# A four-layer transformer chain on one core: attention scores in tiles of three banks and one, keys spread by transfers, half of a modulation on two other engines

## The chip, the cores and the metric

The kernel runs on one NeuronCore of a Trainium2 chip. TensorE (PE in the profile; its weight loads are PEld) does the matrix products, VectorE (DVE), ScalarE (ACT) and GpSimd (POOL) the rest, and SyncE (SP) issues nearly all transfers (DMAs). Matrix products land in PSUM, which the kernel divides into banks of 512 float32 values on 128 partitions; everything else lies in SBUF. Each engine works through its own instructions in order and waits on semaphores for the others; transfers issued by one queue are issued in the order of the program too. The metric is the device time of one execution in microseconds; lower is better. All data are float32.

## What is computed

The input `x` is 128 sequences of 64 tokens with 128 channels, beside a context of the same size and one condition vector for each sequence. Four layers follow one another. The first three are attention with 16 heads of 8 elements; the last one is a mixture of three experts.

```
L0:  x += gate * self_attend(ln(x)*(1+scale)+shift) @ Wp     # 'L0s'
     x += attend(q from ln(x), k and v from the context)@Wp  # 'L0c'
     x += gate * mlp(ln(x)*(1+scale)+shift)
L1:  x += attend(q from ada_ln(x), k, v from ada_ln(ctx))@Wp # 'L1c'
L2:  self attention 'L2s', cross attention 'L2c' (context normalised), mlp
L3:  mixture of experts with a router and a gate
attend: softmax(q k^T / sqrt(8)) v for each head, 64 queries by 64 keys
```

Scales, shifts and gates are linear functions of the condition; they differ from sequence to sequence.

## The kernel before

The 8192 tokens are 16 groups of 512 (8 sequences, called batches in the code); all of `x` stays in SBUF. Attention runs in stages over the groups: L0s and L0c, then the MLP of L0, then L1c, L2s and L2c, then the MLP of L2, then L3. In each attention stage a group goes through three generators whose pieces are interleaved by hand.

`prepare` (line 386) makes a group ready in pieces: load the context, statistics on DVE, normalisation on POOL (in L2c also four pieces `cn` on ACT, L413), a transposition of the normalised tokens by PE into a PSUM tile (`psT`, L342), their modulation or copying into SBUF (`modulated_by_batch`: eight ACT instructions of 64 columns, L359; `copied`, L379), then the key product `pk` (L436), the copy `kT`, and the spread keys `kbd`: four POOL instructions (L444), each multiplying kT by a column of `mask`, so that of each 32 partitions (four heads) only one head's 8 stay non-zero. Then the query product `pq` (L449) with its copy `qT`, and the values `pvv`, `vbd`.

`scores` (line 468) multiplies 32-partition pieces of qT with kbd into one PSUM tile `sc` of four banks, one bank for each four heads, for four batches of a group. DVE reduces it to maxima `mx` (L485) and subtracts them into `e` (L487). `turned` (line 493) transposes half of e by PE into `pp` (two banks, one buffer) and ACT takes the exponential into `eT` (L507); `weighted` multiplies with vbd into `po` (L520) and ACT copies the result to `o` (L528). One value column of vbd is ones, so that po also holds the sums. `finish` (line 530) sends the sums through DRAM to get reciprocals spread over the partitions (`sums`, `rc`, `recs`, `rb`), moves odd heads' results with four transfers `o<-o`, multiplies `oT` on POOL (L557), projects by PE (`py`, L563) and adds to x.

`attend` (line 571) orders it all: step k does the scores of half k, then turns and weighs halves k-1 and k-2, with the pieces of prepare and finish in between. The even step of a pair (u = 0) has on PE: sc, pp, po, pk, py, pp, psT. The odd one: sc, pp, po, pq, pp, pvv, and in cross attention a second psT for the queries. The tiles psT, pk, pq, pvv, po and py share two PSUM banks in turn (`mm`), so each waits until the one two before it has been read. In an attention stage sc has four banks, pp two and mm two, one buffer of sc and of pp.

## Time and profile before

Three runs took 1624.05, 1625.13 and 1627.65 us; the median is 1625.13. The profiled execution took 1626.31 us; its span from the first to the last instruction is 1624.5 us.

| | us | share of the span |
|---|---|---|
| PE busy | 1573.8 | 97% |
| DVE busy | 1240.4 | 76% |
| ACT busy | 1035.5 | 64% |
| POOL busy | 1072.5 | 66% |
| granted TensorE clock, mean | 0.997 | |

Busy time says how long an engine had an instruction under way; PE's ends are modelled, so a busy PE is not a PE at its peak. The groups of instructions give the number, the busy time and the mean duration, then the idle time of the engine before them and who ended it. The chain that ended last is followed back from the end: at each point the work that everything after it waited for.

### The profile page before, as it was taken

How to read it: one execution, taken by the hardware profiler on the slowest of the kernel's cores; microseconds unless marked ns; L12 is line 12 of the kernel's file. 1: busy time of each engine (PE TensorE's matmuls, PEld its weight loads, DVE VectorE, ACT ScalarE, POOL GpSimd, SP SyncE). 2: the span in 40 equal slices, each digit the busy share in tenths (PEclk: the TensorE clock that was granted, in tenths of full speed). 3: DMA queues.
4: the chain of work that ended last, by engine and by line, in shares of the span. 5: the costliest groups of instructions: out<-in, count | busy, mean ns of one | idle time of the engine just before them, and what ended most of it. 6: DMA issues, size and time to landing. Idle time of an engine off the chain costs nothing.

```text
span 1624.5 us, 64028 instructions
## 1 busy us (share of the span) xinstructions
PE 1573.8 (97%) x27842; PEld 1086.8 (67%) x27842; DVE 1240.4 (76%) x1566; ACT 1035.5 (64%) x1710; POOL 1072.5 (66%) x1786
## 2 busy tenths in 40 slices
PE   6999999998999899999999999998999999999998
PEld 4676777776544577776777777776777566666665
DVE  7898998898555688899899889896443566666666
ACT  5788777776433678878888888886334544444443
POOL 6687787766888789887787876775875333333322
PEclk9999999999999999999999999999999999999999
DMA  8334453332111022211334432222533111111100
GB/s 209 85 82 99 107 127 92 83 83 72 55 36 55 16 63 61 72 44 50 90 82 102 104 88 73 62 56 59 130 81 76 31 39 37 40 33 36 34 12 19
DMA packets 146775, 112.65 MB, mean 69 GB/s; under 512 B 36357, under 2 KB 125247, under 8 KB 146495
## 3 DMA queue, kind: packets, MB, share of 16 engines
q1 hardware_dynamic: 146288, 108.53, 26.1%
q8 instruction: 219, 3.59, 0.9%
q14 instruction: 61, 0.50, 0.1%
q10 hardware_dynamic: 207, 0.03, 0.0%
HBM read 83.99 MB, written 14.02 MB: 60 GB/s over the span
## 4 chain that ended last, share of the span: by engine, by line
PE 83%; DVE 12%; ACT 3%; issue 1%; DMA 0%; SPq 0%; DVEq 0%
PE sc L478 10%; PE pp L503 9%; PE po L520 7%; PE ph L693 7%; PE ph L1080 6%; PE ph L1081 6%; DVE e L487 6%; DVE mx L485 6%; PE po L1111 5%; PE psT L342 5%; PE pk L436 5%; PE py L563 4%; PE py L709 4%; PE py L699 3%; PE pvv L459 3%; PE pq L449 3%
## 5 line engine op out<-in xcount | busy, mean ns | idle before, releaser
L507 ACT ACTIVATE eT<-pp 128x1024 f32<-128x1024 f32 x320 | 329.7, 1030 | 160.8 <-PE pp L503 160.7
L485 DVE TENSOR_REDUCE mx<-sc 128x32 f32<-128x2048 f32 x160 | 366.6, 2291 | 83.6 <-PE sc L478 83.6
L487 DVE TENSOR_TENSOR e<-sc,mx 128x2048 f32<-128x2048 f32 x160 | 366.6, 2291 | 5.4
L503 PEld LDWEIGHTS pp<-ident,e 64*128 64x128 f32 x5120 | 183.9, 138 | 140.1 <-ACT eT L507 44.7
L503 PE MATMUL pp<-ident,e 64*128 64x64 f32 x5120 | 227.7, 229 | 7.2 <-DVE e L487 4.7
L444 POOL TENSOR_SCALAR kbd<-kT,mask 128x512 f32<-128x512 f32 x316 | 212.4, 690 | 31.3 <-ACT kT L438 28.3
L372 POOL TENSOR_SCALAR xn<-x,nmu,rs 128x128 f32<-128x128 f32 x508 | 223.6, 453 | 13.3
L557 POOL TENSOR_TENSOR oT<-o,rb 128x512 f32<-128x512 f32 x80 | 102.1, 1276 | 163.5 <-DMA rb<-recs 62.9
L478 PE MATMUL sc<-kbd,qT 32*64 32x256 f32 x5120 | 179.2, 387 | 16.6 <-DVE e L487 15.6
L694 ACT ACTIVATE h<-ph,vec 128x512 f32<-128x512 f32 x128 | 87.3, 687 | 149.9 <-PE ph L693 149.7
L520 PE MATMUL po<-eT,vbd 128*32 128x64 f32 x10240 | 178.1, 221 | 1.4 <-issue 1.3
L1087 ACT ACTIVATE h<-h 128x512 f32<-128x512 f32 x112 | 70.6, 630 | 149.8 <-DVE h L1083 130.9
L520 PEld LDWEIGHTS po<-eT,vbd 128*32 128x32 f32 x10240 | 151.3, 110 | 14.4 <-issue 2.0
L330 POOL TENSOR_TENSOR rs<-rs,nhalf 128x4 f32<-128x4 f32 x128 | 130.2, 1017 | 10.7
L478 PEld LDWEIGHTS sc<-kbd,qT 32*64 32x64 f32 x5120 | 97.7, 131 | 53.0 <-issue 19.6
L1083 DVE TENSOR_TENSOR h<-ph,ab 128x512 f32<-128x512 f32 x112 | 76.9, 687 | 62.6 <-PE ph L1081 62.5
L1116 DVE SCALAR_TENSOR_TENSOR acc<-po,pr,acc 128x128 f32<-128x128 f32 x192 | 67.2, 350 | 44.1 <-PE po L1111 39.6
L1080 PE MATMUL ph<-nx,w 128*128 128x512 f32 x192 | 100.7, 607 | 0.0
L528 ACT COPY o<-po 128x512 f32<-128x512 f32 x160 | 95.7, 598 | 5.1 <-PE po L520 2.0
L1081 PE MATMUL ph<-u,w_ev 128*128 128x512 f32 x192 | 98.9, 597 | 0.0
L1111 PEld LDWEIGHTS po<-w_2o,h 128*128 128x128 f32 x768 | 92.1, 192 | 8.7 <-issue 8.4
L1104 POOL TENSOR_SCALAR g<-g 128x512 f32<-128x512 f32 x16 | 9.9, 622 | 132.1 <-ACT g L1103 132.1
(259 smaller groups left out, 2868.5 us busy)
## 6 DMA issues: line engine op xcount, KB each, us to landing
rb<-recs SPq DMA_DIRECT2D x80, 256.0 KB
c<-in_ctx_dram SPq DMA_DIRECT2D x64, 256.0 KB
o<-o SPq DMA_DIRECT2D x320, 32.0 KB
gt<-gate_L_xcond_sa_proj_w SPq DMA_DIRECT2D x32, 256.0 KB
gt<-gate_L_xcond_W_proj SPq DMA_DIRECT2D x32, 256.0 KB
gt<-gate_L_xcond_W_mlp SPq DMA_DIRECT2D x32, 256.0 KB
x<-in_x_dram SPq DMA_DIRECT2D x16, 256.0 KB
ctxT<-cm SPq DMA_DIRECT2D x16, 256.0 KB
```

What stands on the lines that cost most here:

```text
L330: G.tensor_tensor(rs, rs, nhalf, ALU.pow)
L372: engine.tensor_scalar(xn[:, t, :], src[:, t, :], nmu[:, t : t + 1], rs[:, t : t + 1], ALU.add, ALU.mult)
L444: (V if at.get("first") else G).tensor_scalar(kbd[:, j], by_batch(kT), mask[:, j : j + 1], 1.0, ALU.mult, ALU.mult)
L478: T.matmul(sc[ts(h, L), g, ts(t2, 256)], qT[ts(g, 32), ts(b, L)], kbd[ts(g, 32), :, b, :], start=True, stop=True,)
L485: V.tensor_reduce(mx, sc.rearrange("p g (m k) -> p (g m) k", k=L), AX.X, ALU.max)
L487: V.tensor_tensor(e, sc.rearrange("p g (m k) -> p (g m) k", k=L), mx.unsqueeze(2).broadcast_to([P, 32, L]), ALU.subtract,)
L503: T.transpose(pp[:, h, ts(4 * g2 + 2 * i + t2, L)], e6[ts(h, L), 2 * gg + g2, t2, i], ident[ts(h, L), ts(h, L)],)
L507: S.activation(eT[:, gg], pp, AF.Exp, scale=HD ** -0.5)
L520: T.matmul(po[ts(g, 32), i, ts(2 * t2 + h, L)], at["vbd"][:, 4 * u + 2 * t2 + h, 2 * g + i, :], e7[:, g // 2, h, g % 2, i, t2, :], start=T ...
L1080: T.matmul(ps, wn, d["nx"], start=True, stop=False)
L1081: T.matmul(ps, we, d["u"], start=False, stop=True)
L1111: T.matmul(po[:, ex, :], d[q][:, ts(t, P)], k3["w_2o"][:, q, :], start=r == 0, stop=r == 1)
```

## The change

Six things change together.

1. The order of a head's elements on the partitions: element-major within four heads, instead of head-major, so that a head's rows are every fourth partition. Weights and biases of queries and keys are reordered for it in SBUF at the start (`reorder`, on DVE for L0's self attention, on POOL for the others), and the projection's weights are loaded in two strided transfers. The values' layout, too, is interleaved, and `mask` is computed from the identity.
2. `kbd` becomes two lasting buffers. The first two groups fill them with the mask as before; from then on the zeros stay and four transfers on SP's queue write the 32 partitions of each head position (`spread`).
3. The score tile is three banks (`sc`) and one (`sd`). DVE takes the maxima of sd, then of sc, and subtracts for sc alone. ACT copies sd to SBUF and POOL subtracts there (`rest`), placed after `weighted`.
4. In self attention (but for the first group) ACT modulates four of the eight batches; DVE multiplies the other four in one instruction and POOL adds.
5. In `step`, the key piece of prepare comes before finish's pieces, and in the even step the transposition psT is issued ahead of the second half of `turned`; the instructions that read psT stay behind it.
6. finish: sums in one transfer instead of two, o<-o in one instead of four, rb in two instead of one; the gate tile is loaded earlier in the queue's order, from a table in a layout of longer pieces.

```diff
+    kbds = [
+        Places.ak.tile([P, 4, NB, L], F32, tag=f"kbd{i}", name=f"kbd{i}", bufs=1) for i in range(2)
+    ]
...
+    def reorder(engine, name, n):
+        for i in range(n):
+            t = const([P, P], "gate_bias")
+            cols = w[name][:, 0, ts(i, P)]
+            engine.tensor_copy(t.rearrange("p (g d j) -> p g d j", d=HD, j=4), by_element(cols))
+            engine.tensor_copy(cols, t)
...
+            if half and b >= NB // 2:
+                continue
             if by_dve:
                 V.tensor_scalar(xm[:, ts(b, L)], ps[:, ts(b, L)], m, p, ALU.mult, ALU.add)
             else:
                 S.activation(xm[:, ts(b, L)], ps[:, ts(b, L)], AF.Identity, bias=p, scale=m)
+        if half:
+            dst, src = by_batch(xm)[:, NB // 2 :], by_batch(ps)[:, NB // 2 :]
+            V.tensor_tensor(dst, src, mod(name, scale, s)[:, NB // 2 :], ALU.mult)
+            G.tensor_tensor(dst, dst, mod(name, shift, s)[:, NB // 2 :], ALU.add)
...
+    def spread(kbd, kT):
+        for j in range(4):
+            nc.sync.dma_start(kbd[j:P:4, j].rearrange("p b l -> p (b l)"), kT[j:P:4, :])
...
         yield
+        ps = transposed(psum, cn if cross else xn)
+        if at.get("in_two"):
+            at["open"] = True
+            yield
+            at["open"] = False
         if layer == "L1c":
-            kv_in = modulated_by_batch(pool, transposed(psum, cn), "L1_xcond_Wss_kv", 0, 1, s, "cm")
+            kv_in = modulated_by_batch(pool, ps, "L1_xcond_Wss_kv", 0, 1, s, "cm")
...
-        kbd = pool.tile([P, 4, NB, L], F32, tag="kbd", name="kbd")
-        for j in range(4):
-            (V if at.get("first") else G).tensor_scalar(
-                kbd[:, j], by_batch(kT), mask[:, j : j + 1], 1.0, ALU.mult, ALU.mult
-            )
+        kbd = kbds[i]
+        if turn[0] <= 2:
+            for j in range(4):
+                (V if at.get("first") else G).tensor_scalar(
+                    kbd[:, j], by_batch(kT), mask[:, j : j + 1], 1.0, ALU.mult, ALU.mult
+                )
+        else:
+            spread(kbd, kT)
...
-        sc = psc.tile([P, 4, 512], F32, tag="sc", name="sc")
+        sc = psc.tile([P, 3, 512], F32, tag="sc", name="sc")
+        sd = psc.tile([P, 512], F32, tag="sd", name="sd")
...
-        V.tensor_reduce(mx, sc.rearrange("p g (m k) -> p (g m) k", k=L), AX.X, ALU.max)
         e = pool.tile([P, 32, L], F32, tag="e", name="e")
+        sc = sc.rearrange("p g (m k) -> p (g m) k", k=L)
+        sd = sd.rearrange("p (m k) -> p m k", k=L)
+        V.tensor_reduce(mx[:, 24:32], sd, AX.X, ALU.max)
+        V.tensor_reduce(mx[:, 0:24], sc, AX.X, ALU.max)
         V.tensor_tensor(
-            e, sc.rearrange("p g (m k) -> p (g m) k", k=L),
-            mx.unsqueeze(2).broadcast_to([P, 32, L]), ALU.subtract,
+            e[:, 0:24], sc, mx[:, 0:24].unsqueeze(2).broadcast_to([P, 24, L]), ALU.subtract
         )
-        return e
+
+        def rest():
+            S.copy(e[:, 24:32], sd)
+            G.tensor_tensor(
+                e[:, 24:32], e[:, 24:32], mx[:, 24:32].unsqueeze(2).broadcast_to([P, 8, L]),
+                ALU.subtract,
+            )
+
+        return e, rest
...
-        for j in range(2):
-            nc.sync.dma_start(
-                sums.rearrange("(g i j) t -> j g i t", i=2, j=2)[j], o[16 + j : P : 32, :, :]
-            )
+        nc.sync.dma_start(sums.rearrange("(m i) t -> m i t", i=2), o[1:P:16, :, :])
+        if not cross:
+            gt = gate_tile(pool, s, at["wp"])
...
-        for g in range(4):
-            nc.sync.dma_start(o[32 * g + 16 : 32 * g + 32, 0, :], o[32 * g : 32 * g + 16, 1, :])
+        nc.sync.dma_start(o[1:P:2, 0, :], o[0:P:2, 1, :])
...
-        nc.sync.dma_start(rb, recs.unsqueeze(1).broadcast_to([16, HD, NT]))
+        for i in range(2):
+            r = recs.rearrange("(m i) t -> i m t", i=2)[i]
+            nc.sync.dma_start(rb[i:P:2, :], r.unsqueeze(1).broadcast_to([8, HD, NT]))
...
                 weighted(pools, past["at"], past["u"], past["eT"])
+            if rest:
+                rest()
             if u == 0:
+                go(prep, i + 1)
                 go(fin, i - 2)
                 go(prep, i + 4)
-                go(prep, i + 1)
                 go(fin, i - 3)
+                if i + 2 < n:
+                    ats[i + 2]["in_two"] = True
+                go(prep, i + 2)
             else:
                 go(prep, i + 1)
             if last:
                 turned(pools, last["e"], last["eT"], 1)
             if u == 0:
-                go(prep, i + 2)
+                if i + 2 < n and ats[i + 2].get("open"):
+                    go(prep, i + 2)
                 go(prep, i + 3)
...
         condition()
+        reorder(V, "L0_xcond_qkv_w", 2)
         ahead_1(0, 0)
```

## The prediction

> **What bounds the kernel now.** I read the page first, then a table of busy time by stage, then the chain that ended last inside one stage of each kind, then the timeline where that chain left TensorE. The page (unit busy lines, and the chain's shares):
>
> ```profile
> PE 1573.8 (97%) x27842; PEld 1086.8 (67%) x27842; DVE 1240.4 (76%) x1566; ACT 1035.5 (64%) x1710; POOL 1072.5 (66%) x1786
> PE 83%; DVE 12%; ACT 3%; issue 1%; DMA 0%; SPq 0%; DVEq 0%
> L485 DVE TENSOR_REDUCE mx<-sc 128x32 f32<-128x2048 f32 x160 | 366.6, 2291 | 83.6 <-PE sc L478 83.6
> L487 DVE TENSOR_TENSOR e<-sc,mx 128x2048 f32<-128x2048 f32 x160 | 366.6, 2291 | 5.4
> L444 POOL TENSOR_SCALAR kbd<-kT,mask 128x512 f32<-128x512 f32 x316 | 212.4, 690 | 31.3 <-ACT kT L438 28.3
> ```
>
> PE is nearly always busy, yet DVE owns 12% of the chain and ACT 3%: some stages are not bound by PE. Four stretches, one per attention layer (first number after the window is its length, then PE, PEld, DVE, ACT, POOL busy): inside L0's cross attention, L1, L2's self attention, L2's cross attention.
>
> ```profile
> 240.00:360.00 120.00, 119.95 (x3080) 87.53 (x3072) 107.99 (x81) 87.57 (x120) 85.02 (x133) 1.00 0.32 88
> 620.00:720.00 100.00, 98.60 (x2494) 71.64 (x2492) 89.88 (x62) 79.00 (x146) 88.30 (x144) 1.00 0.24 59
> 760.00:900.00 140.00, 135.72 (x3566) 99.50 (x3562) 126.87 (x95) 113.32 (x209) 108.43 (x159) 1.00 0.36 89
> 940.00:1090.00 150.00, 149.26 (x3861) 109.17 (x3857) 134.10 (x100) 125.00 (x198) 104.65 (x162) 1.00 0.29 71
> ```
>
> L0's cross stage has no idle PE at all; L2's self stage has 4.3 us idle in 140, with DVE 91% busy. A group of tokens takes two steps (four of its eight batches each), so 160 steps in all. I took step lengths as the distance between successive starts of L487: cross stages of L0 and L2 alternate 5.92 and 6.09 us, self stages 5.94 and 5.98, L1 5.92 and 6.33. Chains, self stage first, then L1:
>
> ```profile
> 887.39 1.13 PE sc L478 x32
> 888.55 2.30 DVE mx L485
> 890.87 2.30 DVE e L487
> 893.31 1.12 PE sc L478 x32
> ...
> 657.45 0.66 PE pp L503 x16
> 658.13 1.02 ACT eT L507
> 659.15 1.27 ACT cm L359 x5
> 660.50 1.03 ACT cm L359 x3
> 661.57 1.12 PE pq L449 x2
> ```
>
> In self, a loop of scores, maxima and subtraction fills a step: sc can't start until e is done, since there is one sc tile. In L1, the second turning of an even step (pp), its exponential, then eight small modulations on ACT release the PSUM tile that pq needs; natural PE order would have had pq 0.25 us earlier. In the cross stages of L0 and L2 the chain is PE alone: pieces of 1.05 (sc), 0.64 (pp, twice), 1.03 (po), then 1.06, 0.92 and 0.59 (pk, py, psT) in the even step, 5.93 in all, or 1.06, 1.08 and 0.59 (pq, pvv, psT) in the odd one, 6.09. Self lacks the odd psT: its PE need is 5.50 against the 5.98 it takes.
>
> **The change, part by part.**
>
> *Scores in 3+1 banks.* DVE's two 2291 ns passes become 512, 1536 and 1536 columns. L347 reads 512 columns in 691 ns; with 2291 at 2048 that is 1.042 ns a column plus 158, so 691 + 1758 + 1758 = 4.21 us for 4.58, less one further gap of 0.03: 0.34 saved in the loop. Self's odd steps go 5.98 → 5.64 (PE would allow 5.50). I count 27 of them (11 in L0 after the start, 16 in L2 and at the end of L1): -9.2. Even self steps can only go to PE's 5.92: -0.5. Some eight steps at stage ends, which lack other PE work and run at 5.90 to 5.98, gain 0.3 each: -2.4. Cross steps gain nothing here, PE covers them. Sum -12.1; -13 without the further gap, -6 if the three passes saved only half.
>
> *The copy by ACT and subtraction by POOL.* ACT gains 160 copies like L528 (598 ns, about 0.48 back to back). It waits for DVE's maxima of that bank (1.9 us into the step) and stands after the o copy, whose turn ends about 3.3 in; kT starts at 3.9, so it fits before it, and the bank is free long before the next scores. In L2's cross stage ACT is busy 10.1 us of 12.1 a group and then 11.0: little slack, which the moved psT, below, uses up. POOL gains 160 subtractions; with a broadcast operand the nearest row is L348, 1042 ns (without one L557, 1276). That is 2.1 us a group (up to 2.55), and the result is needed by the second pp of the next step, over 5 us later. An oT that waits for rb now stands before the even step's subtraction; it is through 2.6 us into that step, before the data are there: nothing on the path.
>
> *Keys by transfer.* POOL loses four L444 per group, 2.76 us, so its load barely moves. SP gains four issues per group, 0.62 each by the o<-o row (2.47 for four), 0.33 at the least; it loses one sums and three o<-o issues and gains one rb. They wait for kT, about 4.6 us into the even step, so the last is issued at about 6.5 to 7.1. The rb transfer took at most 3.9 us from issue (1000.46) to its reader (oT at 1004.38): keys land by 11.0 at the latest, needed at 11.9. Behind them in the queue now stands recs (6.3 before, 7.1 now), then rb twice: oT up to 1.1 later, which took until 2.6 us into the next even step; py wants it at 3.8. Both covered, by about 1 us; cost 0, and bounds 0 to +0.3 a group.
>
> The Trainium skill, "DMA: Bandwidth & Descriptors", section "Anatomy of one DMA", fits transfers issued by GpSimd with a fixed cost of about 2.0 us each, which speaks against four small ones in place of one pass. The rb row, issued by SP, shows up to 3.9 in all, so the cover is thinner than by the page; by the page the keys would land some 1.7 us sooner, and the sum is the same by both.
>
> *Half of self's modulation on DVE and POOL.* ACT does four of eight L359 pieces (2.47 us → 1.24), DVE one 256-column pass (0.42), POOL one add (about 0.55). In a self even step DVE then holds 4.24 + 0.54 (reciprocal) + 0.63 (y) + 0.42 = 5.83, under 5.92: no cost. pq no longer waits for ACT there.
>
> The page "GPSIMD Engine Reference", section "Engine selection", speaks against two-input work on GpSimd, about twice VectorE's time: 1.38 us for 512 columns, where L348 shows 1042 ns. By it POOL's load would stay as before and the sum too.
>
> *The even step's psT moves ahead of its second pp.* This is the costly part. pp now ends the step, 0.59 later, and its exponential with it (start about 0.07 after pp, 1.02 long). Three consequences:
> - L1: the chain pp, eT, cm, pq shown above is already the bound; its modulations are still eight pieces behind the exponential. So it grows by psT's 0.59, the odd step 6.33 → 6.92. I count 11 such steps: +6.5 (0 if something else released pq, +8 with the first groups).
> - L2 cross: ACT's queue after that exponential holds cm and four cn pieces (L413) before the next step's first exponential, which releases the second pp. From the timeline, the exponential of an even step's second pp, cm, the cn pieces and the exponential of the odd step's first pp:
>
> ```profile
> 1008.66 1.02 ACT L507 ACTIVATE eT<-pp 128x1024 f32<-128x1024 f32 x1 [0.85 <-PE pp L503]
> 1009.58 0.58 ACT L379 COPY cm<-psT 128x512 f32<-128x512 f32 x1
> 1010.04 1.66 ACT L413 ACTIVATE cn<-c,ctx_nb,ctx_rs 128x128 f32<-128x128 f32 x4
> 1011.60 1.01 ACT L507 ACTIVATE eT<-pp 128x1024 f32<-128x1024 f32 x1
> ```
>
> The second ends 3.95 after the first starts. Shifted, it ends 4.05 us into the odd step; pp's turn comes at 3.78. +0.3 for 15 groups: +4.5 (0 to +7).
> - Every group: only sc (1.05) is left between this pp and the next step's first pp, which needs the exponential done, at 0.07 + 1.02 + 0.06 = 1.15. +0.1. L0's cross stage pays it 16 times, +1.6 (0 to +3); in self the DVE loop covers it, in the two others it is in the wait counted.
>
> *The start.* qkv's two column blocks are reordered on DVE before the first statistics: four copies of about 0.28 (as xn's 1.12 for four), held until the qkv weights land. The previous weights' reader started at 5.8, these land by about 6.3 (bounds 5.8 to 7.5); statistics end at 8.2 in place of 5.45: +2.75. Then group 1's modulation waits for DVE's e of step 0 (5.5 us after sc), +0.42, then POOL's add, before pk; the second sc comes about 8.3 after the first in place of 5.97: +2.35. ACT's halved pieces bring the first exponential 1.3 earlier, which the 7.33 us step after it waited for: -1.3. Sum +3.8 (2 to 6.5). The later reorderings on POOL (16 copies of about 0.45 in L0, where POOL had 29 us idle in 140) and more DMAs for the weights: 0.
>
> *Fewer and longer gate, sums and o transfers*: off the path, 0.
>
> Sum: -12.1 + 6.5 + 4.5 + 1.6 + 3.8 = +4.3. The profiled execution took 1626.31 us, a span of 1624.5 and 1.8 around it, 1.2 above the median of the runs; so 1630.6 by it, or 1629.4 from the median 1625.13. I say 1629.5.
>
> **Rivals.**
> - *The moved psT costs nothing.* If ACT starts these exponentials as early as before, L1, L2 cross and L0 cross stay: -12.1 + 3.8 = -8.3, 1617. For it: PE's ends are modelled, and the two idle waits at pq are only 0.2 each. Against: the chain of L1 goes through exactly this pp.
> - *Transfers late.* SP's queue holds keys, recs and rb in order; one recs landing in L2's cross stage took 2.9 us in place of 1.5. From 1 us more than I put, py (or sc) waits in every group; 0.3 us over on 76 groups is +23: 1652. Against: SP issues about 7.5 us in 12 now and hardly more after.
> - *The DVE loop doesn't shorten.* If a third pass costs 0.3 us more than the fit, or another instruction (reciprocal, y, the new pass) fills the gap, only the losses remain: 1625 + 16 = 1641.
>
> **How the numbers follow.** Sum as worked out: 0.53 (1623 to 1636); first rival 0.20 (1613 to 1622); transfers 0.12 (1640 to 1665); loop 0.15 (1636 to 1645). A measurement can tell about 0.2%, 3.3 us. Faster than 1621.9 holds most of the first rival and a little of the main case: 0.22. Within: 0.23, the lower half of the main case. Slower: 0.55. Range 1614 to 1645, which leaves out the late transfers and the far end of the first rival.
>
> **What would show it.** Step starts: self odd steps near 5.6, L1 odd near 6.9, L2 cross odd near 6.4, L0 cross odd 6.2. In L1, pq's wait for ACT cm grows to 0.8. In L2 cross, the second pp waits for ACT eT. A first sc near 18.5 us in place of 15.7. POOL's oT never the last before py. I am wrong if L1's odd steps stay at 6.33, or if PE waits for kbd's transfers.

## The result and the profile after

The changed kernel takes 1687.43 us in the median (four runs, 1683.17 to 1691.15), the kernel before beside it 1626.39 (four runs). The ratio is 1.0375, with a 95% interval of 1.0344 to 1.0406: slower by 61 us. The forecast was 1629.5, and its range ended at 1645. The profiled execution took 1685.92 us, its span 1684.1, with a mean granted clock of 0.995 (0.997 before); the difference is worth about 3 us, so the clock is not the cause.

The page after: busy time of PE, the chain's shares, and the groups that make the scores' maxima and differences.

```profile
PE 1581.5 (94%) x27844; PEld 1089.3 (65%) x27844; DVE 1180.4 (70%) x1766; ACT 1073.4 (64%) x1746; POOL 1054.4 (63%) x1681
PE 57%; ACT 9%; DMA 4%; issue 3%; POOL 2%; DVE 1%; SPq 1%; ACTq 0%; POOLq 0%; DVEq 0%
L574 DVE TENSOR_TENSOR e<-sc,mx 128x1536 f32<-128x1536 f32 x160 | 281.2, 1757 | 5.5
L573 DVE TENSOR_REDUCE mx<-sc 128x24 f32<-128x1536 f32 x160 | 279.6, 1747 | 0.0
L580 POOL TENSOR_TENSOR e<-e,mx 128x512 f32<-128x512 f32 x160 | 167.2, 1045 | 62.5 <-ACT e L579 61.1
L572 DVE TENSOR_REDUCE mx<-sd 128x8 f32<-128x512 f32 x160 | 110.2, 689 | 102.1 <-PE sd L562 100.3
```

Every piece has the length that the forecast gave it (689, 1747 and 1757 ns against 691 and 1758; the subtraction on POOL 1045 against 1042). DVE holds 60 us less than before, and PE, with 7.7 us more of work, is now 94% busy and not 97%: the time is in waits. The chain after is followed back only to 383 us, so its shares, which are of the whole span, leave out L0's two attention stages and can't be set beside those of before one by one. From L1's first subtraction to the last one of L2's cross stage, which both chains cover, DVE's part of the chain goes from 110 us to 5, ACT's from 37 to 143 and that of the transfers (DMA) from 0 to 53. DVE's part is larger than that in truth: its hold on the scores stands under another name, as shown below.

The same four stretches as before (length, then PE, PEld, DVE, ACT and POOL busy): L0's cross stage, L1, L2's self stage, L2's cross stage.

```profile
240.00:360.00 120.00, 114.50 (x2914) 82.34 (x2902) 93.76 (x95) 91.86 (x133) 75.51 (x108) 1.00 0.34 106
620.00:720.00 100.00, 94.18 (x2410) 68.24 (x2411) 78.00 (x71) 83.38 (x159) 81.30 (x126) 1.00 0.26 81
760.00:900.00 140.00, 125.18 (x3324) 91.72 (x3318) 111.41 (x120) 104.90 (x176) 97.44 (x138) 1.00 0.30 92
940.00:1090.00 150.00, 142.59 (x3663) 102.63 (x3648) 118.03 (x121) 126.82 (x212) 100.97 (x142) 1.00 0.34 101
```

No engine but PE is over 85% busy in any of them, and PE, which had no idle time in L0's cross stage, has 5.5 us in 120 there and 14.8 in 140 in L2's self stage.

I took the length of stages from the starts of DVE's subtraction (L487 before, L574 after): the first one, then the distance to the first one of the next stage, in the two cross stages to the last one of their own; "MLP" is from there to L1's first, "end" what is left of the span. The last three rows are experiments that make one part of the change alone (below). The MLP's 2 us were not followed.

```
us                    first  L0 self  L0 cross    MLP     L1  L2 self  L2 cross    end    span
before                 19.3    193.5     187.3  146.8  194.6    192.2     187.2  503.7  1624.5
after                  22.9    210.7     197.6  148.9  203.2    205.3     192.3  503.3  1684.1
difference             +3.6    +17.2     +10.3   +2.1   +8.6    +13.1      +5.1   -0.4   +59.6
psT ahead alone (e7)   19.2    196.9     187.8  148.3  201.8    196.0     190.4  500.8  1641.2
half alone (e8)        20.6    207.6     186.2  146.8  197.8    203.0     186.1  500.7  1648.8
keys alone (e9)        21.8    202.7     199.5  150.7  199.0    195.0     192.1  504.0  1664.9
```

Step by step, self groups took 5.94 and 5.98 us (even step, odd step) and take 7.26 and 5.53; L1's took 5.92 and 6.33 and take 5.79 and 7.00; L2's cross groups took 5.92 and 6.09 and take 5.78 and 6.49. L0's cross steps are irregular, from 5.57 to 8.32.

**A self group.** DVE's last two instructions of one even step and the first of the next, then ACT's in the same stretch, each from the timeline (start, length, engine, line):

```profile
836.55 0.63 DVE L660 TENSOR_TENSOR y<-py,gt 128x512 f32<-128x512 f32 x1
839.63 0.42 DVE L426 TENSOR_TENSOR xm<-psT,mod_L_xcond_W_mod 128x256 f32<-128x256 f32 x1 [2.45 <-ACT xm L423]
839.97 0.68 DVE L572 TENSOR_REDUCE mx<-sd 128x8 f32<-128x512 f32 x1
```

```profile
837.39 1.02 ACT L601 ACTIVATE eT<-pp 128x1024 f32<-128x1024 f32 x1 [2.06 <-PE pp L597]
838.31 1.29 ACT L423 ACTIVATE xm<-psT,mod_L_xcond_W_mod 128x64 f32<-128x64 f32 x4
```

DVE is free at 837.18, and psT was there at 836.71 (PE makes it ahead of the pp whose exponential begins at 837.39). But DVE's half (L426) is let go only when ACT's four pieces are done, and these stand behind that exponential. So DVE stands for 2.45 us, with the next maxima (L572) queued behind L426 and the next subtraction, which frees the score tile, behind those. DVE's waits between 760 and 900 us (total, times, longest) have it as their largest sum:

```profile
DVE xm L426 <- ACT xm L423: 19.9, 11, 2.4
```

The late subtraction then holds PE. A group earlier, DVE's subtraction and PE's next scores:

```profile
828.89 1.76 DVE L574 TENSOR_TENSOR e<-sc,mx 128x1536 f32<-128x1536 f32 x1
830.75 0.44 PE L562 MATMUL sc<-kbd,qT 32*64 32x256 f32 x3 [1.22 <-issue]
```

The scores start 0.10 us after the subtraction's end, and so they do in each regular group of the self stages. The profile puts PE's 1.22 us down to "issue" and not to DVE, which is why the chain after shows so little of DVE.

**L1.** The chain of work there, which is the one shown of before with psT (656.00) ahead of pp, and the wait that ends it:

```profile
656.00 0.52 PE psT L404 x4
656.52 0.66 PE pp L597 x16
...
657.20 1.03 ACT eT L601
658.23 0.82 ACT cm L423 x3
...
660.65 1.12 PE pq L532 x2
```

```profile
PE pq L532 <- ACT cm L423: 5.0, 8, 0.6
```

**SP's queue in L0's cross stage.** The waits of SP between 240 and 360 us, of the kernel before and then of the kernel after (about ten groups each):

```profile
SPq L542 <- DMA sums<-o: 18.0, 10, 2.4
SPq L554 <- DMA recs<-rc: 15.9, 10, 2.6
SPq L549 <- DVE rc L547: 11.1, 9, 1.8
```

```profile
SPq L635 <- DMA sums<-o: 27.0, 9, 3.6
SPq L646 <- DMA recs<-rc: 17.4, 10, 2.9
```

Before, SP waited in turn for the sums to land in DRAM, for DVE's reciprocals, and for those to land. After, the wait for DVE's reciprocals is gone: when SP has issued the keys, the reciprocals have long been there, and they leave late. SP now runs without slack from one group to the next.

### The profile page after: what moved, and what is told of

It is laid out like the page before. It is cut to its first block, busy times and chain, and to the rows that moved or that the text cites. A ratio compares the mean times of both kernels' runs of the same rounds, so it can differ in the third digit from the quotient of the medians.

```text
span 1684.1 us, 64352 instructions
## 1 busy us (share of the span) xinstructions
PE 1581.5 (94%) x27844; PEld 1089.3 (65%) x27844; DVE 1180.4 (70%) x1766; ACT 1073.4 (64%) x1746; POOL 1054.4 (63%) x1681
## 4 chain that ended last, share of the span: by engine, by line
PE 57%; ACT 9%; DMA 4%; issue 3%; POOL 2%; DVE 1%; SPq 1%; ACTq 0%; POOLq 0%; DVEq 0%
PE ph L792 7%; PE ph L1179 6%; PE ph L1180 6%; PE po L1210 5%; PE pp L597 5%; ACT eT L601 4%; PE py L808 3%; PE psT L404 3%; PE py L798 3%; PE po L614 3%; PE py L655 3%; PE sc L562 3%; PE pk L516 2%; PE pvv L542 2%; DMA rb<-recs 2%
## 5 line engine op out<-in xcount | busy, mean ns | idle before, releaser
L574 DVE TENSOR_TENSOR e<-sc,mx 128x1536 f32<-128x1536 f32 x160 | 281.2, 1757 | 5.5
L573 DVE TENSOR_REDUCE mx<-sc 128x24 f32<-128x1536 f32 x160 | 279.6, 1747 | 0.0
L440 POOL TENSOR_SCALAR xn<-x,nmu,rs 128x128 f32<-128x128 f32 x508 | 225.3, 459 | 13.2
L580 POOL TENSOR_TENSOR e<-e,mx 128x512 f32<-128x512 f32 x160 | 167.2, 1045 | 62.5 <-ACT e L579 61.1
L572 DVE TENSOR_REDUCE mx<-sd 128x8 f32<-128x512 f32 x160 | 110.2, 689 | 102.1 <-PE sd L562 100.3
L562 PE MATMUL sd<-kbd,qT 32*64 32x256 f32 x1280 | 178.1, 390 | 0.0
L579 ACT COPY e<-sd 128x512 f32<-128x512 f32 x160 | 96.9, 606 | 5.3 <-DVE mx L572 5.3
```

The source lines that it names most:

```text
L440: engine.tensor_scalar(xn[:, t, :], src[:, t, :], nmu[:, t : t + 1], rs[:, t : t + 1], ALU.add, ALU.mult)
L562: T.matmul((sd if g == 3 else sc[:, g])[ts(h, L), ts(t2, 256)], qT[ts(g, 32), ts(b, L)], kbd[ts(g, 32), :, b, :], start=True, stop=True,)
L573: V.tensor_reduce(mx[:, 0:24], sc, AX.X, ALU.max)
L574: V.tensor_tensor(e[:, 0:24], sc, mx[:, 0:24].unsqueeze(2).broadcast_to([P, 24, L]), ALU.subtract)
L580: G.tensor_tensor(e[:, 24:32], e[:, 24:32], mx[:, 24:32].unsqueeze(2).broadcast_to([P, 8, L]), ALU.subtract,)
```

## Experiments

Ratios are to the kernel before on the same chip, with their 95% intervals.

### The half of the modulation, and where psT stands

Theory after the first reading: the self groups lose by DVE's wait for ACT's pieces, L1 and the cross stages by psT's place as forecast, the rest by something in the transfers. Rival: the new transfers make all stages late.

*DVE's half first* (e1): DVE's multiplication and POOL's addition are issued ahead of ACT's four pieces.

```diff
+        if half:
+            dst, src = by_batch(xm)[:, NB // 2 :], by_batch(ps)[:, NB // 2 :]
+            V.tensor_tensor(dst, src, mod(name, scale, s)[:, NB // 2 :], ALU.mult)
+            G.tensor_tensor(dst, dst, mod(name, shift, s)[:, NB // 2 :], ALU.add)
         for b in range(NB):
...
-        if half:
-            dst, src = by_batch(xm)[:, NB // 2 :], by_batch(ps)[:, NB // 2 :]
-            V.tensor_tensor(dst, src, mod(name, scale, s)[:, NB // 2 :], ALU.mult)
-            G.tensor_tensor(dst, dst, mod(name, shift, s)[:, NB // 2 :], ALU.add)
```

> The changed kernel with one order reversed: in self's modulation DVE's multiplication and POOL's add of the upper four batches are issued before ACT's four pieces, so that ACT waits for DVE in place of DVE for ACT. Theory 1 (DVE's pass L426 waits for ACT's pieces, which stand behind the exponential of the step's last pp, and the next maxima stand behind it on DVE): self's even steps go from 7.26 us back to about 5.95 on some 30 groups, -39, a median near 1648 (1642 to 1656). Rival (self's even steps are long because the transfers of keys make rb, oT and py late): no change beyond 5 us, 1682 to 1692.

*No half at all* (e2): ACT makes all eight pieces.

```diff
-                half=not at.get("first", False),
```

> The changed kernel without the division of self's modulation: ACT does all eight pieces again. Theory 1: DVE waits for nothing here, but ACT's eight pieces stand behind an exponential that the moved transposition has made 0.59 late, so pq waits as in L1: self steps 5.9 and 6.35 in place of 7.26 and 5.53, -0.54 on 30 groups, near 1671. Rival (late transfers): self's even steps stay near 7.2, 1687 or more.

*psT behind the second pp, as before* (e3), and *both e1 and e3* (e4):

```diff
-                if i + 2 < n:
-                    ats[i + 2]["in_two"] = True
-                go(prep, i + 2)
...
-                if i + 2 < n and ats[i + 2].get("open"):
-                    go(prep, i + 2)
+                go(prep, i + 2)
```

> The changed kernel with the even step's transposition psT back behind the second pp. As predicted for the moved psT: L1's odd steps 7.0 to 6.35 (14 of them, -9), L2 cross 6.49 to 6.2 (-4), L0 cross -1.5. Theory 1 adds: ACT's pieces end 0.59 earlier, so DVE's wait in self shrinks by as much, even steps 7.26 to 6.7 on 30 groups, -17; together near 1656. Rival (late transfers): only the first three, near 1673. If the moved psT costs nothing: 1687.

> Both edits, DVE's half first and psT behind the second pp. Theory 1: -39 and -14.5, near 1633, so that what is left against the kernel before is the start (+7) and L0's cross attention (+12), less the shorter DVE loop (-12). Rival (late transfers in self): near 1672.

| | median, us | ratio | regular self steps | L1 steps |
|---|---|---|---|---|
| after | 1687.43 | 1.0375 (1.0344 to 1.0406) | 7.26, 5.53 | 5.79, 7.00 |
| e1, DVE first | 1665.32 | 1.0235 (1.0197 to 1.0274) | 5.8, 5.6 | as after |
| e2, all on ACT | 1674.42 | 1.0288 (1.0258 to 1.0318) | 5.86, 6.34 | as after |
| e3, psT late | 1667.53 | 1.0249 (1.0215 to 1.0283) | 6.74, 5.53 | 5.85, 6.41 |
| e4, both | 1664.67 | 1.0213 (1.0174 to 1.0253) | 5.9, 5.53 | 5.85, 6.41 |

e2 came within 4 us of its number; e1 and e3 came out between theory and rival. The mechanisms show where they were put: with DVE first, the 7.26 falls to 5.8; with psT late, L1's 7.00 falls to 6.41, and the self step loses half a microsecond of its wait. But the sum doesn't follow: e4 has both repaired and was expected near 1633, and its time is hardly under that of either alone. In it PE's py waits 37.7 us for oT on POOL (30 times, up to 4.5 us), against 17.6 us in the changed kernel, and single steps take 10 to 12 us. It looks as if what had been hidden behind the longer steps came out: the rows of the denominators are late. So the theory's "rest by transfers" was more than a rest.

*Each part alone, added to the kernel before* (e7: the three edits that put psT ahead; e8: the half, with ACT's pieces first):

> The kernel before with one thing changed: the even step's psT ahead of the second pp. By the predicted mechanism: L1's 11 steps of 6.33 become 6.92 (+6.5), L2 cross +0.2 on 15 groups (+3), L0 cross +1.6; and self, where ACT keeps all eight pieces, gets L1's wait too: odd steps 5.98 to 6.33 on 28 groups (+10). Near 1646 (1638 to 1652). If the moved psT costs nothing: 1625.

> The kernel before with one thing changed: self's modulation divided as in the changed kernel, ACT's four pieces issued first. Theory 1 (DVE's pass waits for ACT's pieces and the next maxima stand behind it): DVE can start the maxima 7.1 us after the even step's start, now only at 8.1 (exponential to 6.4, four pieces to 7.7, DVE's 0.42): +1.0 on 29 groups, near 1654 (1645 to 1660). If the wait is harmless: 1618 to 1628.

e7 took 1646.32, ratio 1.0114 (1.0097 to 1.0130); e8 1650.74, ratio 1.0144 (1.0129 to 1.0159). L1's odd steps are 6.88 in e7 and L2's cross odd steps 6.38. In e8 the even self steps are 6.80. Its DVE, from the timeline (the maxima at 840.23 belong to the next step):

```profile
839.89 0.43 DVE L364 TENSOR_TENSOR xm<-psT,mod_L_xcond_W_mod 128x256 f32<-128x256 f32 x1 [0.85 <-ACT xm L361]
840.23 2.28 DVE L492 TENSOR_REDUCE mx<-sc 128x32 f32<-128x2048 f32 x1
```

So the wait doesn't need psT ahead, the new score tiles or the transfers: the half as it was written costs 24 us on the kernel before by itself, 4.8 of them in the second step of all.

### The keys' transfers

*The keys and the channel order alone* (e9): the changed kernel with four banks taken whole by DVE, no half, and psT in its old place. The reordering at the start, the merged transfers of item 6 and the key piece's place in `step` stay in it, so it isn't the keys by themselves.

```diff
-        sc = psc.tile([P, 3, 512], F32, tag="sc", name="sc")
-        sd = psc.tile([P, 512], F32, tag="sd", name="sd")
+        sc = psc.tile([P, 4, 512], F32, tag="sc", name="sc")
...
-        return e, rest
+        return e, None
```

> The kernel before with the reordered channels, the block form of the keys made by four transfers and the changed order of the head's rows alone: scores stay in four banks that VectorE takes whole, ScalarE makes all the modulation, psT is made where it was. Theory (the four issues of the keys' transfers stand on SP's queue ahead of a finish's reciprocals and rows, so the attention's output comes late wherever a group has a gate or rows to issue too): 1645 to 1665 us, the excess in L0's cross steps (+10 to +24 between the steps k32 and k64) and L2's cross steps (+3 to +8), and +7 at the start; self steps as before within 0.05 us, and the chain of waits shows py waiting for oT in L0's cross stage. Rival (the lateness of oT comes from POOL, where the subtractions of the fourth bank keep a finish's additions and oT waiting, and the transfers cost what I forecast, nothing): 1629 to 1633 us, all of it at the start, and py waits for oT no more than before.

1664.67 us, ratio 1.0227 (1.0204 to 1.0251): the dearest part of all, +38 us, of which 2.5 come before the first subtraction. In L0's cross stage PE's weight loads wait for oT, which the list of before doesn't have:

```profile
PEld py L643 <- POOL oT L637: 14.5, 9, 2.6
```

PE doesn't wait for the keys: a new group's scores start there at most 0.24 us after the subtraction that frees their tile, as most did before the change. Only at the start of L0's self stage did they twice come about 2 us late (2.5 and 1.9, after 1.5 and 1.0 before), and once by 1.0 in L1. Self steps were expected as before; L0's self stage has single ones of 6.8 to 8.5 us. One round of SP's queue in L0's cross stage, first before the change, then in e9 (start, time the issue took, line):

```profile
257.22 1.19 SPq L538 DMA_DIRECT2D sums<-o  x2
259.81 0.33 SPq L542 DMA_DIRECT2D rc<-sums  x1
260.19 3.22 SPq L545 DMA_DIRECT2D o<-o  x4
263.66 0.37 SPq L549 DMA_DIRECT2D recs<-rc  x1
265.24 0.56 SPq L554 DMA_DIRECT2D rb<-recs  x1
265.85 1.54 SPq L394 DMA_DIRECT2D c<-in_ctx_dram  x1
267.48 0.46 SPq L420 DMA_DIRECT2D ctxT<-cm  x1
```

```profile
261.53 0.60 SPq L619 DMA_DIRECT2D sums<-o  x1
265.71 0.32 SPq L623 DMA_DIRECT2D rc<-sums  x1
266.08 0.53 SPq L625 DMA_DIRECT2D o<-o  x1
266.66 3.40 SPq L456 DMA_DIRECT2D kbd<-kT  x4
270.17 0.52 SPq L629 DMA_DIRECT2D recs<-rc  x1
272.24 1.32 SPq L634 DMA_DIRECT2D rb<-recs  x2
273.61 0.44 SPq L468 DMA_DIRECT2D c<-in_ctx_dram  x1
274.15 0.45 SPq L499 DMA_DIRECT2D ctxT<-cm  x1
274.69 0.60 SPq L619 DMA_DIRECT2D sums<-o  x1
```

The keys' four issues stand between rc's load and recs. Two landings that SP must sit out are in each round: from sums to rc (1.4 us between issues before, 3.6 here, where the sums are one transfer and not two) and from recs to rb (1.2 and 1.6). Issues and landings together fill the 13.2 us from one sums to the next. Over the whole stretch from 240 to 360 us SP's issues hardly grow, since three of o<-o and one of sums are gone: 6.5 us a group before, 7.2 in e9. What grows more is the wait for the sums to land, 1.8 us a time before and 3.3 in e9 (18.0 us in ten, 29.7 in nine).

*The same issues with nothing waiting for them* (e13), *with a sixteenth of the bytes* (e14), *and two of them in place of four* (e16): to the kernel before, masks and channel order untouched, transfers of kT into a piece of DRAM that nobody reads.

```diff
+        if turn[0] > 2:
+            unread = dp.tile([P, 512], F32, tag="unread", name="unread", bufs=2)    # e14, e16: [P, 32]
+            for j in range(4):                                                      # e16: range(2)
+                nc.sync.dma_start(unread[j:P:4, :], kT[j:P:4, 0:512])               # e14, e16: 0:32
```

> The kernel before with four transfers of kT added for each group on SP's queue, behind the keys' masks, into DRAM that nobody reads: the same issues and bytes as the keys' transfers, and nothing waits for them. Theory (their place on SP's queue makes the denominators' rows late): 1640 to 1665 us, with py waiting for oT in L0's cross stage as in e9. Rival (what costs in e9 is the wait for the keys themselves, or the other layout): 1624 to 1630 us.

> As the run with unread transfers, but of 32 columns of kT and not 512: the same four issues a group, a sixteenth of the bytes. Theory by the number of issues: the time of the full-width run within 5 us. Rival by the bytes in the rings: within 5 us of the kernel before, 1622 to 1632 us, where the full-width run is slow.

> The run of narrow unread transfers with two of them a group and not four. Theory (SP's queue in L0's cross stage of the kernel before has only 11.1 us of waiting for VectorE's reciprocals in 9 groups to give, 1.2 us a group, and an issue takes 0.6: two issues of 1.2 us fit, four of 2.4 do not): L0's cross steps between k32 and k64 take 334 to 340 us, against 355 with four, and the whole kernel 1627 to 1637 us. Rival (each issue delays the rows by its own length wherever it stands): half of what four cost, 1641 to 1645 us.

```
us                        median   ratio (95% interval)       first  L0 self  L0 cross     L1  L2 self  L2 cross
four, full width (e13)   1658.61   1.0196 (1.0176 to 1.0217)   19.9    196.7     205.5  195.9    195.8     190.9
four, narrow (e14)       1658.65   1.0185 (1.0166 to 1.0204)   20.3    196.2     205.9  199.0    196.9     190.6
two, narrow (e16)        1629.61   1.0017 (1.0005 to 1.0028)   19.0    194.2     188.1  196.6    192.4     186.1
```

(The expectation of e16 counts to one step later, "between k32 and k64", which adds the MLP's 147 us or so: 336 measured.) Three things are shown. The bytes don't matter: a sixteenth of them costs the same. Nothing has to wait for the transfers: their place on the queue is enough. And the cost isn't proportional: two issues cost 3 us, four cost 31, most of it in L0's cross stage. SP's waits there say why. In e13 the landings are left and the wait for DVE's reciprocals is gone, and in e16 some of it is left:

```profile
SPq L558 <- DMA recs<-rc: 14.5, 9, 3.0
SPq L546 <- DMA sums<-o: 12.8, 10, 2.0
```

```profile
SPq L558 <- DMA recs<-rc: 16.1, 10, 3.2
SPq L546 <- DMA sums<-o: 13.3, 11, 1.3
SPq L553 <- DVE rc L551: 4.5, 5, 1.4
```

The landings themselves are no longer than before (in e13 1.3 and 1.6 us a wait, before 1.8 and 1.6), so what was added to the queue is the time of the issues. On one point the expectation of e13 missed: py hardly waits for oT there (2.6 us between 240 and 360 us). DVE's reciprocals wait 13.3 us for the sums to come back, x's addition stands behind them, and PE's po waits 8.5 us for that addition to free its PSUM bank. So e13 shows what four issues on this queue cost, but not the path by which the changed kernel pays.

I read the slack of the queue as the wait for something that is not itself a link of the queue's own loop: 11.1 us for DVE's reciprocals in nine waits, 1.2 us a group. Two issues take 1.2 us, four take 2.4. In L2's self stage of the kernel before the same wait is 22.6 us in 12 groups, and another 19.6 stand ahead of the sums: 3.5 us a group, and four issues cost only 3.6 us in the 16 groups of e13.

*Masks on POOL again in the three cross stages* (e5), or *the keys' transfers of L0's cross stage issued by ACT's queue* (e6), both from e4:

```diff
-        if turn[0] <= 2:
+        if turn[0] <= 2 or cross:                          # e5
...
-            spread(kbd, kT)
+            spread(kbd, kT, nc.scalar if layer == "L0c" else None)    # e6
```

> The kernel with DVE's half first and psT late, and in the three cross stages the keys spread by POOL's mask again (self keeps the transfers). Theory 2 (the four key transfers stand ahead of recs in SP's queue and fill it, so that rb, oT and py come late in the cross stages, and each late py stops PE): L0 cross loses its 20 to 24 us of irregular steps and L2 cross its 7, near 1634 (1628 to 1642). Rival (what is left comes from ACT's copies and POOL's subtractions): no gain, 1660 or more.

> The kernel with DVE's half first and psT late, and in L0 cross alone the key transfers issued by ACT's queue in place of SP's: the same transfers and bytes, another queue. Theory 2, if it is the order and the issuing time in SP's queue: L0 cross loses some 20 us, near 1645. If it is the load on the transfer engines themselves: no change, 1660 to 1668. ACT pays four issues a group, 2 us, where it is busy 77%, so PE may lose up to 0.3 a group (+5).

e5: 1642.85, ratio 1.0099 (1.0082 to 1.0116). L0's cross stage is back at 185.4 us, from 208.9 in e4, and L2's at 185.0, so in the changed kernel too it is the keys' transfers that cost these stages. The merged transfers are still there; without the keys' issues the wait for the reciprocals is back on SP's queue in L0's cross stage, 2.5 us a group:

```profile
SPq L641 <- DVE rc L639: 24.7, 10, 3.6
```

L1, though, has 204.4 and keeps the whole just above the 1628 to 1642 expected: there POOL already normalises the context and now masks and subtracts too, 97 us busy in 100, and its even steps go to 7.0.

e6: 1670.99, ratio 1.0274 (1.0254 to 1.0294), and L0's cross stage is no better (209.4 against e4's 208.9). By its time alone this would fit a load on the transfers themselves, against which e14 stands. SP's queue is relieved, yet ACT itself issues the transfers now, and its exponential stands behind them:

```profile
ACT eT L601 <- DMA kbd<-kT: 25.2, 9, 3.3
```

The Trainium skill, "DMA: Bandwidth & Descriptors", section "Issuing engines are not separate DMA queues", says that issuing from several engines saves only the sequencer's time, "which is usually small relative to the DMA itself". In these rows an issue takes about 0.60 us, less than a landing that SP waits for (1.3 to 3.6 us); but e13 beside e14 shows that the bytes were not the cost, so on a full queue the small time is the one that counts. And e6 shows no gain where ACT issues in SP's place.

*The gate's place* (e11: e4 with a self group's gate tile loaded behind rb), and a *mixture* (e10: e11 with masks on POOL in L0's and L2's cross stages, and the second and third self group modulated by ACT alone):

```diff
-        if not cross:
-            gt = gate_tile(pool, s, at["wp"])
         rc = pool.tile([P, L], F32, tag="rc", name="rc")
...
+        if not cross:
+            gt = gate_tile(pool, s, at["wp"])
         yield
```

> The kernel of e4 with the gate tile of a self group (512 KB) issued behind the rows of the denominators and not ahead of them. Theory (the gate's bytes stand ahead of the denominators' rows in the transfer rings, and of them on SP's queue, which makes oT late at irregular steps of the self stages): the irregular self steps of 7 to 12 us shrink to under 7 us and the time falls from 1664.7 to about 1645 to 1655 us, with L0's cross steps unchanged. Rival (the lateness comes from the keys' issues alone, whatever stands in the rings): 1660 to 1670 us, and the irregular steps stay.

> The kernel of e4 (VectorE's half of the modulation ahead of ScalarE's pieces, psT behind the second pp) with four edits: in L0's and L2's cross stages the block form of the keys is made by POOL's masks as before, in L0's self and L1 by transfers; the gate tile is loaded behind the rows of the denominators; the first two self groups after the first are modulated by ScalarE alone. Theory: L0's cross steps back at before's 5.9 and 6.1 us as in e5 (334 us between k32 and k64, against 358 in e4), L1's as in e4 (5.9 and 6.4), L2's cross at 97 us between k128 and k144, self steps 5.9 and 5.5 us with what irregular long steps remain: 1625 to 1645 us, and under 1620 only if the irregular steps of the self stages go. Rival (the irregular steps stay wherever four transfers per group share SP's queue with gate and rows): 1640 to 1650 us.

Both came out slower than either of their expectations. e11 took 1702.06, ratio 1.0456 (1.0437 to 1.0476): the self stages grow by 15.5 us each against e4. e10 took 1670.21, ratio 1.0276 (1.0251 to 1.0301), with the cross stages at 185.9 and 185.3 as meant, and the self stages at 213.0 and 210.8. In e10's L2 self stage POOL waits for the gate itself:

```profile
POOL x L651 <- DMA gt<-gate_L_xcond_W_proj: 7.6, 8, 1.5
```

Its 512 KB are wanted straight after oT, so the early place of the changed kernel is the better one of the two. What makes single self steps 6 to 12 us long in e4 beyond this was not taken apart further; in a kernel without the keys' transfers such steps are gone (next).

### The divided scores without the transfers

*e12*: the kernel before, with the scores in three banks and one in the self stages only; masks on POOL, all modulation on ACT, psT in its old place, old channel order. In the cross stages DVE subtracts from both parts. The last addition of a self group goes from POOL to DVE, to make room for the subtractions. *e15*: the same, with copy and subtraction on ACT and POOL in L0's and L2's cross stages too.

```diff
+        shared = at["layer"] != "L1c" and not at.get("first")        # e12: the self layers alone
-        sc = psc.tile([P, 4, 512], F32, tag="sc", name="sc")
+        sc = psc.tile([P, 3, 512], F32, tag="sc", name="sc")
+        sd = psc.tile([P, 512], F32, tag="sd", name="sd")
...
+        last = mx[:, 24:32].unsqueeze(2).broadcast_to([P, 8, L])
+        if not shared:
+            V.tensor_tensor(e[:, 24:32], sd, last, ALU.subtract)
+            return e, None
+        def rest():
+            S.copy(e[:, 24:32], sd)
+            G.tensor_tensor(e[:, 24:32], e[:, 24:32], last, ALU.subtract)
...
-            G.tensor_tensor(xs[s], xs[s], y, ALU.add)
+            V.tensor_tensor(xs[s], xs[s], y, ALU.add)
```

> The kernel before (its channel order, its masks on POOL, all modulation on ScalarE, psT where it was) with the scores in three banks and one, the one copied by ScalarE and less its maxima by POOL in the self stages alone; in the cross stages VectorE takes both parts; the last addition of a self group's finish is made by VectorE. Theory (the division of the scores is worth what the self steps of e4 show, 11.4 us a group where the path is regular, and all that is irregular comes from the keys' transfers): self steps 5.9 and 5.5 us without long ones, cross steps as before within 0.05 us, start as before: 27 groups by 0.45 us or so less, 1612 to 1618 us. Rival (POOL, which holds some 11.3 us a self group here, makes the irregular steps): self groups at 12 us or more, 1627 us or over.

> The run with masks on POOL and the divided scores in the self stages, with the divided scores in L0's and L2's cross stages too (copy by ScalarE, subtraction by POOL), so that only L1's fourth bank is left to VectorE. Theory (those two stages are bound by TensorE, and VectorE's four instructions were what made their even steps 5.98 and not 5.92): cross groups of 12.0 us and not 12.1 there, 1622 to 1627 us. Rival (POOL's subtractions make the borders between self and cross longer): 1628 to 1634 us.

e12: 1627.79, ratio 0.9997 (0.9986 to 1.0008), no gain where 1612 to 1618 was expected. e15: 1617.84, ratio 0.9948 (0.9934 to 0.9962), better than its own expectation of 1622 to 1627 and than both kernels. Busy times in L2's self stage of e15, in the columns used above:

```profile
760.00:900.00 140.00, 137.62 (x3636) 100.14 (x3632) 126.94 (x131) 125.00 (x240) 129.34 (x184) 1.00 0.41 95
```

No self step is over 6.4 us outside the start. The keys' transfers are then the likely cause of the steps of 7 to 12 us, since e9 has some of up to 8.5 with them and without the half; but e15 also leaves out the half and the merged transfers, so this isn't shown for the longest. The odd steps are 5.6 to 5.8 and the even ones 5.9 to 6.3, not 5.5 and 5.9. PE, DVE, ACT and POOL are each 89 to 98% busy, and I didn't find which of them holds a step. The self stages gain 2.6 and 3.8 us on the kernel before. In e12 the cross stages gave all of it back: DVE's four instructions make their even steps 5.98 instead of 5.92, and the steps around the change from self to cross 6.5 to 7.0. e15 takes that load off DVE, and the cross stages have 186.4 and 184.9 us against 189.5 and 189.4 (187.3 and 187.2 before).

## Why the prediction was wrong

**The half of the modulation: the step that failed first.** It said: "In a self even step DVE then holds 4.24 + 0.54 (reciprocal) + 0.63 (y) + 0.42 = 5.83, under 5.92: no cost." The sum of DVE's work is right, each term within 0.1 us. What it left out is a wait: ACT and DVE both read psT, in the order of the program, and ACT's pieces stand behind the exponential. DVE holds the next maxima while it waits for work that it could have done before. The even self step went to 7.26 and not 5.92, +1.3 us in 27 groups. e8 shows 24 us for it alone, and e1 that the order of two statements decides it. What is queued behind a new wait was asked for POOL and SP, and not for DVE.

The Trainium skill, "PSUM — Partial Sum Buffer", section "PSUM bank collisions raise a hardware error", says that two engines must not access one PSUM bank in the same partitions at the same time, two readers included, and that software puts a dependency between them, ScalarE and VectorE too. psT's 512 columns are one bank, and the rows agree: DVE's L426 starts 0.03 us after ACT's L423 ends, though both only read. No run here lets the two read together. By that sentence a half of the columns of a one-bank tile on another engine is not parallel work; it moves work from one queue to the other, in series.

**The keys: cost 0 with bounds of 0 to +0.3 a group. The second step that failed.** With the channel order and the merged transfers (e9) they measured +38 us; four issues a group on the kernel before (e13) measured +31, 0.4 us a group over 78 groups. The mechanism was the one of the rival "transfers late", given 0.12 and 1652 us; its argument against, "SP issues about 7.5 us in 12 now and hardly more after", is where the forecast went wrong. That the issues hardly grow was right (they are 6.5 us a group in L0's cross stage before, not 7.5, and 7.2 in e9), but issue time alone doesn't fill a queue: two landings that SP sits out, 3.4 us a group, belong to its loop too. With them, 1.1 us of waits for the reciprocals (the 11.1 over ten groups) and 1.0 for pieces of other engines, the 12 us of a group were full; the wait for the reciprocals was what SP had to give. The lines were in the trace of before. In e9 SP issues 0.7 us more a group and sits out landings for 5.2 in place of 3.4. The larger part of this is at the sums, which as one transfer land 3.3 us after SP starts to wait, against 1.8 for the two; "Fewer and longer gate, sums and o transfers: off the path, 0" left that out. The merging was not tested by itself: e5, which keeps it, has L0's cross stage at 185.4 us, so it costs nothing there without the keys' issues. The keys themselves were in time, as worked out ("needed at 11.9"), but for three groups of e9; what came late was oT, "covered, by about 1 us".

**psT ahead of the second pp: right.** Forecast: L1's odd steps 6.33 → 6.92, L2's cross 6.09 → 6.4, L0's cross → 6.2. Measured 7.00, 6.49 and 6.23 to 6.30 in the regular steps; e7, with this part alone, has 6.88, 6.38 and 6.18. The wait of pq for ACT's cm is 0.6 and was given as 0.8. Alone it costs 19 us, not the 12.6 of the forecast, because on the kernel before it also lengthens odd self steps to 6.3 (pq waits 16.9 us there for ACT's eight pieces); in the changed kernel the half spares this, as was said ("pq no longer waits for ACT there").

**The divided scores: right in size, and without a place to show.** Self's odd steps are 5.53 where 5.64 was said. The work of the three passes is as fitted. But one step of a group won 0.45 and the other lost 1.3. What the division can bring on this kernel is seen in e15: 9 us, against 12.1 in the sum.

**Copy by ACT and subtraction by POOL: no cost, right** in cross and self stages; the profile after shows no wait of PE for POOL's subtraction.

**The start: inside its bounds.** The first scores began at 18.41 us (18.5 said), the second 9.73 us after them (8.3 said, 5.97 before) and the third 6.32 after those (7.33 before, 1.3 less said). By the third that is +5.4 us, where 3.8 was said, with 2 to 6.5 as bounds. The second term was short, and it is the half's: e8, which has the half alone, needs 10.73 there, and e9, which leaves it out, 6.08.

**The signs to look for.** "POOL's oT never the last before py" was named as what must hold, and failed; "PE waits for kbd's transfers" was named as what would refute, and didn't happen in the changed kernel. The parts alone sum to 81 us (19 + 24 + 38), and the kernel lost 61, with 9 to 12 gained by the scores. My reading is that where one part makes a step longer, another's delay hides in it, and that e1, e3 and e4 come out within 3 us of each other for this reason; py's wait for oT, 17.6 us in the changed kernel and 37.7 in e4, speaks for it, but how much hides where was not measured.

## What to carry to other kernels

Before a queue gets more to issue, add its issue times and the landings it sits out into one loop for each group, and take the wait for something outside that loop as its slack: 1.2 us here, which took two issues for 3 us in the whole kernel and four for 31. Where two engines read one PSUM bank, as here psT, expect them one after the other, in the order of the program; give the first place to the engine with the earlier free time, and look at what is queued behind the one that waits. When a kernel's stages have different limits, a gain for one of them (here DVE's in the self stages) should be bought only in those stages where the payer has room: e15 left L1 alone and won 0.5%.

## What the runs showed of the hardware that was not expected

- A transfer's issue on SP took 0.59 us in the median whether its rows were 2 KB or 128 B (e13 and e14), and the whole kernel's time was the same for both (1658.61 and 1658.65 us).
- A stall of PE can cost more than its length. In e4 PE waited 3.19 us for oT and went on at a granted clock of 0.50; its py took 2.08 us in place of 1.08, the pp after it 1.11 in place of 0.71, psT 1.12 in place of 0.66, and so on until about 842.7. Busy times of that stretch; the granted clock is the figure before the last two:

```profile
834.00:838.00 4.00, 1.48 (x7) 1.48 (x8) 1.46 (x2) 0.05 (x1) 2.68 (x3) 0.74 0.31 103
838.00:842.00 4.00, 4.00 (x55) 2.81 (x54) 1.12 (x2) 1.77 (x4) 3.95 (x5) 0.50 0.19 64
```

In e4's clock record the half-clock stretches ahead of the program's end are 3.41 or 6.83 us long, and each of its five steps of 10 us and more has one, the first step of all among them. This is part of why a few late rows made single steps of 11 to 12 us out of waits of 2.4 to 4.5.
